# A graph layer over 1.65 million edges: every edge gathered in plain groups, no separate treatment of a node's edge to itself

## The chip, the cores and the metric

The kernel runs on one core of a Trainium2 chip. The metric is the device time of one execution in microseconds. The kernel before takes 18567.04 us, the median of 9 runs from 18510.53 to 18612.28 us. The engines are named as the profile names them: PE is the matrix engine (PEld its loading of weights), DVE the vector engine, ACT the scalar engine, POOL the engine that issues the indirect gathers, SP the one that issues most plain transfers.

## The reference, cut to what matters

There are 50,000 nodes of 160 numbers each (64 scalars and 32 three-vectors) and 1,650,000 edges sorted by their destination: 800,000 random pairs in both directions, and one edge from each node to itself. Because the sort is stable, a node's edge to itself is the last of its edges. Each edge has 4 attributes.

```python
ss, vv = (s[src], v[src])                  # the source's row of x
out0 = C0 * (ss * e0 @ W1 + dot * INV3 @ W2)
p3 = (ss @ W3)[:, :, None] * e1[:, None, :] * INV3
p4 = jnp.einsum('eui,uw->ewi', vv * e0[:, :, None], W4) * INV3
p5 = jnp.einsum('eui,uw->ewi', jnp.cross(vv, e1[:, None, :]), W5) * INV6
m = concat(out0, C1 * (p3 + p4 + p5))      # one message per edge
m_agg = segment_sum(m, dst, num_segments=n)
h = m_agg through Ws and Wv                # 160 x 160, block by block
x = layernorm(x + (x + relu(h)))
```

A message is linear in the source's row and linear in the four attributes. So the sum over a node's edges is the sum over k of (the sum of attribute k times the source's row) times a fixed 160 x 160 matrix, and the kernel gathers rows, forms these weighted sums by matrix products, and multiplies with the folded weights afterwards.

## The kernel before, in words

**Groups and pairs.** A group is `G` = 6 units of 128 edges, 768 edges, which touch at most `W` = 32 consecutive nodes. Two groups are a pair (`PG`), four a chunk (`QG`), twenty a super-group (`SG`). The main loop at the end of `tile_gnn_resnorm` runs over pairs, 1044 of them.

For each pair `gather` (line 319) issues 12 indirect transfers on POOL, one per unit, each of which brings 128 rows of x into the tile `xg`. The pool of `xg` has 4 buffers of one pair each: POOL can run 48 gathers ahead of the matrix products that read them, and then waits until PE has finished the oldest pair. `spread` (329) makes, on DVE, the weighted selection `ha` of 128 edges by 4 x 32 columns for each unit. `group_sums` (356) multiplies `ha` with the gathered rows into `ps` in PSUM, one matrix product per unit. A float32 product is two PE instructions and two weight loads in the records. `turn_sums` (370) transposes `ps` into `sums` on DVE.

**Behind a chunk.** `apply_weights` (598) multiplies a chunk's `sums` with the folded weights `BWk`, 5 products into `phc`, and ACT copies the result to `hp`. For each of 391 blocks of 128 nodes `block` (677) adds the chunks that touch it with 4 or 5 products by a 0/1 matrix into `phb`; then come the residual, the normalisation and the store. These products come from a task list, and `work` lets about one of them through after each gathered unit's product, so on PE they stand between the `ps` products in program order. Their PSUM tiles (`phc`, `phb`, `yx`, `ptx`) share one pool of two buffers.

**The edge of a node to itself.** Its row of x is the node's own, which is loaded in order anyway. From group 100 (`NH`) on the kernel therefore does not gather it. `pack` (431) reads rows of `L` = 790 edges, marks those whose source is their destination, and squeezes them out with predicated copies on DVE. The rest go to a DRAM array `edges` of 6 numbers an edge, and the attributes of the squeezed-out ones to an array `selves`, in 1994 stores of 18.5 KB and 1992 of 0.5 KB on SP. `load` (248) then reads super-groups from `edges` in one transfer of 360 KB. For every block, `ahead` (619) loads the rows of x and the stored attributes, `turned` (644) transposes the rows with two products into `ptx`, `own` (656) makes 8 products `yx` with the weights, and DVE adds them up into `t` with the attributes as factors; `block` adds `t` to `phb`. The first 100 groups are read from the inputs as they are (three transfers and a conversion on ACT), with the edges to itself among them.

**Order.** PE, DVE, ACT and SP keep the order in which the program writes their instructions. `after_pair` puts each step of later work at a pair: for a block whose last chunk ends at pair p, the load at p - 7 (`AHEAD`), `turned` at p - 4, `own` at p - 2, `block` at p + 4. At the end a few flags are read; if a group had spanned more than 32 nodes, a second, slower pass would follow.

```python
for j in range(n - len(others)):                     # gather, 319
    got.append(nc.gpsimd.indirect_dma_start(out=xg[:, j, :], ...).ins)
...
mm = nc.tensor.matmul(ps[:, j // G, :], ha[:, j].rearrange("p k w -> p (k w)"), xr, ...)   # group_sums, 356
```

Of the kernel before, what the change touches and what calls it, by code (L numbers as in the profile page):

```python
# [39 lines left out]
F32 = mybir.dt.float32  # L40
I32 = mybir.dt.int32
# [29 lines left out]
HELP = {}  # L71
HEAD = 100
BP = 2
RP = 128
RS = 16
KM = 31

ROWS = {ET.SP: 32, ET.Activation: 16}


def plan(n_nodes, n_edges):

    nblk = 125
    assert n_nodes % nblk == 0
    assert W == FB
    nb = n_nodes // nblk
    again = 9

    per_unit = P * n_nodes / n_edges
    group = max(g for g in range(1, 17)  # L90
                if g == 1 or (g + 0.2) * per_unit + 1 + 5 * math.sqrt(g * per_unit * per_unit / P) <= W)
    head = math.ceil(min(HEAD, n_edges / (group * P)) / SG) * SG
    eh = head * group * P
    row = group * P + math.floor(per_unit * group * (1 - n_nodes / n_edges))
    assert row * n_nodes / n_edges + 5 * math.sqrt(row * n_nodes / n_edges / 16) < KM

    far = math.ceil(6 * math.sqrt(n_edges) / 2 * n_nodes / n_edges) + 2
    rows = math.ceil((n_edges - eh) / row) + 2
    ngroups = math.ceil((n_edges - n_nodes + eh * n_nodes / n_edges + far) / (group * P))
    assert eh + (rows - 1) * row - n_nodes + eh * n_nodes / n_edges - far >= ngroups * group * P  # L100
    units = P * math.ceil(max(math.ceil(n_edges / P) + again - 1, math.ceil((eh + rows * row + 1) / P)) / P)
    return nblk, nb, again, group, units, ngroups, row, head, rows, far
# [3 lines left out]
def tile_gnn_resnorm(ctx: ExitStack, tc: tile.TileContext, x, src, dst, attr, W1, W2, W3, W4, W5, Ws, Wv, out, n_edges):  # L106
    nc = tc.nc
    N = x.shape[0]
    NBLK, NB, GA, G, NU, NG, L, NH, NR, FAR = plan(N, n_edges)
    NCH = math.ceil(NG / QG)  # L110
    EH = NH * G * P
# [94 lines left out]
    def near(c):  # L206
        p = c * QG * G * P
        return p / degree if p <= EH else EH / degree + (p - EH) / (degree - 1)

    step = QG * G * P / (degree - 1)  # L210
    cuts = sorted({0, NH // QG, NCH} | {round(i * NCH / 10) for i in range(10)})
    bounds = []
    for c0, c1 in zip(cuts, cuts[1:]):
        t = min((near(c) / N for c in range(c0, c1 + 1)), key=lambda t: abs(t - 0.5))
        off = 5 * math.sqrt(n_edges * max(0, t * (1 - t))) / (degree - 1) + 10
        bounds += [(-off, 0.75 * step + W + off)] * (c1 - c0)
# [9 lines left out]
    with tc.tile_pool(name="once", bufs=1) as once, tc.tile_pool(name="raw", bufs=2) as rawp, \  # L226
            tc.tile_pool(name="idx", bufs=2) as idxp, tc.tile_pool(name="rows", bufs=4) as rowp, \
            tc.tile_pool(name="far", bufs=3) as farp, \
            tc.tile_pool(name="ops", bufs=3) as op, tc.tile_pool(name="sums", bufs=4) as sump, \
            tc.tile_pool(name="hp", bufs=alive + 4) as hpp, tc.tile_pool(name="node", bufs=3) as np_, \  # L230
            tc.tile_pool(name="ahead", bufs=5) as aheadp, tc.tile_pool(name="outs", bufs=3) as outp, \
            tc.tile_pool(name="psC", bufs=1, space=PSUM) as psC, tc.tile_pool(name="psK", bufs=2, space=PSUM) as psK, \
            tc.tile_pool(name="psP", bufs=1, space=PSUM) as psP, tc.tile_pool(name="psA", bufs=2, space=PSUM) as psA, \
# [11 lines left out]
        offsets = {}  # L245
        evict = nc.vector.tensor_copy if ET.Activation in HELP else nc.scalar.copy

        def load(s):
# [3 lines left out]
            if g0 >= NH:  # L252
                p0 = g0 * G * P - EH
                r6 = rawp.tile([P, P, 2 + NK], F32, name="r6")
                dq.dma_start(r6[:n].rearrange("u p c -> u (p c)"),
                             edges[0, p0 * (2 + NK):(p0 + n * P) * (2 + NK)].rearrange("(u q) -> u q", u=n))
                return s, n, None, r6[:n, :, 0], r6[:n, :, 1], r6[:n, :, 2:]
# [6 lines left out]
            return s, n, ri, None, None, ra[:n]  # L264

        def cast(loaded):
            s, n, ri, sf, df, af = loaded
            if ri is not None:
                rf = rawp.tile([P, 2, P], F32, name="rf")
                begun.append(nc.scalar.copy(rf[:n], ri[:n]))  # L270
                sf, df = rf[:n, 0, :], rf[:n, 1, :]
            if HELP:

                ro = rawp.tile([P, P], I32, name="ro")
                nc.scalar.mul(ro[:n], sf, 4.0 * D)
                offsets[s] = ro
            return s, n, sf, df, af
# [41 lines left out]
        def gather(placed, u, n, others):  # L319

            xg = rowp.tile([P, PG * G, D], F32, name="xg")
            got = []
            for j in range(n - len(others)):
                got.append(nc.gpsimd.indirect_dma_start(  # L324
                    out=xg[:, j, :], out_offset=None, in_=x,
                    in_offset=bass.IndirectOffsetOnAxis(ap=placed[0][:, u + j:u + j + 1], axis=0)).ins)
            return [xg[:, j, :] for j in range(n - len(others))] + others, got
# [28 lines left out]
        def group_sums(p, rows, ha):  # L356
# [3 lines left out]
            rows, got = rows  # L360
# [13 lines left out]

        halves = ((0, L // 2), (L // 2, L))
        C = 2 + NK
        npacks = math.ceil(NR / RP)
        real = math.ceil((n_edges - EH) / L)
        LW = math.ceil(L / W) * W

        def row_start(r):

            lo, hi = (math.floor(r * L * (1 - 1 / degree)) - 2 * FAR - 2, math.ceil(r * L * (1 - 1 / degree)) + 2 * FAR + 2)
            return (max(lo, 0), hi if r else 0), (max(math.floor((EH + r * L) / degree) - FAR - 2, 0),
                                                  math.ceil((EH + r * L) / degree) + FAR + 2)

        edges = dram.tile([1, (row_start(NR - 1)[0][1] + L) * C], F32, name="edges")
        selves = dram.tile([1, (row_start(NR - 1)[1][1] + W) * NK], F32, name="selves")
        edge_bytes = edges.bitcast(U8).rearrange("o f -> (o f)")
        self_bytes = selves.bitcast(U8).rearrange("o f -> (o f)")  # L390
        rows_stored = [0]

        def row_table(tmp):

            NT = npacks * RP
            raw = tmp.tile([1, NT], I32, name="raw")
            at = tmp.tile([1, NT], F32, name="at")
            node = tmp.tile([1, NT], F32, name="node")
            nc.vector.memset(raw[:, NR:], 0)
            with nc.allow_non_contiguous_dma(reason="one number of each row"):  # L400
                dq.dma_start(raw[:, :NR], dst[EH:EH + NR * L].rearrange("(o r e) -> o r e", o=1, e=L)[:, :, 0])

            nz = math.ceil((row_start(0)[1][1] + W) / P)
            zeros = tmp.tile([P, nz * NK], F32, name="zeros")
            nc.vector.memset(zeros, 0.0)
            dq.dma_start(selves[0, 0:P * nz * NK].rearrange("(p f) -> p f", p=P), zeros)
            nc.gpsimd.iota(at, pattern=[[L, NT]], base=0, channel_multiplier=0, allow_small_or_imprecise_dtypes=True)
            most, least = math.ceil(EH / degree) + FAR, max(math.floor(EH / degree) - FAR, 0)
            nc.vector.tensor_scalar(node, raw, float(N), float(-most), op0=ALU.min, op1=ALU.add)
            nc.vector.scalar_tensor_tensor(node, at, 1 / degree, node, op0=ALU.mult, op1=ALU.min)  # L410
            nc.vector.tensor_scalar(node, node, float(most - least), None, op0=ALU.add)
            nc.vector.scalar_tensor_tensor(node, at, 1 / degree, node, op0=ALU.mult, op1=ALU.max)
            nc.vector.tensor_scalar(node, node, float(least), None, op0=ALU.add)

            nc.vector.tensor_copy(spots[:, :NT], node)
            nc.vector.tensor_copy(node, spots[:, :NT])

            nc.vector.scalar_tensor_tensor(at, at, node[:, 0:1], node, op0=ALU.add, op1=ALU.subtract)

            moved = raw.bitcast(F32)  # L420
            nc.vector.scalar_tensor_tensor(moved[:, :NR], raw[:, :NR], float(N), node[:, :NR],
                                           op0=ALU.min, op1=ALU.subtract)
            nc.vector.tensor_reduce(strayed[0:1, 0:1], moved[:, :NR], axis=AX.X, op=ALU.min)
            nc.vector.tensor_reduce(strayed[0:1, 1:2], moved[:, :NR], axis=AX.X, op=ALU.max)
            by_round = spots.rearrange("o (c j t i) -> o c j t i", c=npacks, j=RS, t=2)
            for t, (what, width) in enumerate(((at, C), (node, NK))):
                nc.vector.tensor_scalar(by_round[:, :, :, t, :],
                                        what.rearrange("o (c i j) -> o c j i", c=npacks, j=RS), float(4 * width), None,
                                        op0=ALU.mult)

        def pack(c):

            r0 = c * RP
            n = min(RP, NR - r0)
            e0 = EH + r0 * L
            e = slice(e0, e0 + n * L)
            steps, T = [], {}

            def read():
# [658 lines left out]
```

## Time and profile before

| What | Value |
|---|---|
| median of 9 runs | 18567.04 us |
| the profiled execution, its time | 18546.95 us |
| its span, first to last instruction | 18544.8 us |
| gathers on POOL | 12522, 946 ns busy each |
| first and last gather's start | 8.4 and 18502.2 us |
| PE matrix products, records | 41633, of them `ps` 25044, `yx` 6256, `phc` 5220, `phb` 3474, `ptx` 782 |
| DVE busy | 6445.8 us |
| ACT busy | 486.5 us |
| mean granted PE clock | 0.667 of full speed |

The profile is one execution taken by the hardware profiler. Its page gives busy times by engine, the chain of work that ended last, and groups of like instructions. Other views are drawn from the same trace: the waits (who sat idle, and what ended it), one tile's instructions, and the timeline. The span has no stages that differ: between 1000 and 18000 us every stretch of 2000 us holds between 1343 and 1374 POOL instructions. "Remote" in a wait means that the profile found no instruction whose end fits the semaphore that was waited for.

### The profile page before, as it was taken

The page shows a single profiled execution, that of the slowest core. Times are in us where ns is not written, and L with a number is a line of the kernel's source. Part 1 is how long each engine was busy: PE and PEld are TensorE (multiplying, and loading weights), DVE is VectorE, ACT ScalarE, POOL GpSimd, SP SyncE. Part 2 cuts the span into 40 slices and gives each one's busy share as a digit, 9 for nine tenths or more (in the row PEclk, how much of TensorE's full clock was granted, in tenths as well). Part 3 has the DMA queues.
Part 4 walks back from the last instruction along what each step waited for, and adds up shares of the span by engine and source line. Part 5 has one row for each costly group of instructions (what it writes and reads, how often), then busy time and mean ns, then how long its engine had stood idle before and what let it go on. Part 6 is the DMA issues. An engine that isn't in the chain of part 4 may idle for free.

```text
span 18544.8 us, 122717 instructions
## 1 busy us (share of the span) xinstructions
PE 8636.7 (47%) x41633; PEld 7739.0 (42%) x41634; DVE 6445.8 (35%) x11070; ACT 486.5 (3%) x1392; POOL 11853.4 (64%) x12536
## 2 busy tenths in 40 slices
PE   4444444444444454544445444454444445444444
PEld 3334444443444444444344444444444344444434
DVE  4332433423333242332333334233342423323322
ACT  0000000000000000000000000000000000000000
POOL 6666666666666666666666666666666666666665
PEclk6666666666666666666666666666666666666666
DMA  2222222222222222222222222222222222222222
GB/s 69 71 61 71 63 65 68 62 71 60 66 68 64 71 63 66 69 64 68 61 66 69 62 70 63 73 62 66 69 63 70 61 71 62 62 69 60 65 62 54
DMA packets 797538, 1215.93 MB, mean 66 GB/s; under 512 B 271491, under 2 KB 575800, under 8 KB 792918
## 3 DMA queue, kind: packets, MB, share of 16 engines
q0 software_dynamic: 601056, 1026.60, 22.5%
q1 hardware_dynamic: 194410, 180.15, 3.3%
q8 instruction: 330, 5.41, 0.1%
q14 instruction: 302, 2.47, 0.0%
q10 hardware_dynamic: 1440, 1.29, 0.0%
HBM read 1135.77 MB, written 71.40 MB: 65 GB/s over the span
## 4 chain that ended last, share of the span: by engine, by line
another core or an unknown queue 41%; issue 18%; PE 16%; DVE 10%; POOL 9%; DMA 1%; ACT 1%; DVEq 0%; SPq 0%; ACTq 0%; POOLq 0%
POOL xg L324 9%; PE ps L362 9%; DVE ha L336 2%; PE phb L684 2%; PE phc L603 2%; PE yx L665 2%; DVE hot L333 1%; DVE sums L372 1%; DMA xg<-in_x,si 1%; DVE prow L534 1%; DVE t L673 1%; DVE hot L638 0%; DVE pra L534 0%; DVE t L671 0%
## 5 line engine op out<-in xcount | busy, mean ns | idle before, releaser
L324 POOL DMA_INDIRECT xg<-in_x,si x12522 | 11849.2, 946 | 6649.1 <-issue 3633.5
L362 PE MATMUL ps<-xg,ha 128*128 128x160 f32 x25044 | 6542.7, 364 | 3452.6 <-issue 3115.2
L362 PEld LDWEIGHTS ps<-xg,ha 128*128 128x128 f32 x25044 | 5115.2, 241 | 3905.0 <-issue 3516.2
L372 DVE STREAM_TRANSPOSE sums<-ps 128x320 f32<-128x320 f32 x1044 | 533.7, 511 | 5392.0 <-remote 4064.8
L665 PE MATMUL yx<-BWh,xT 80*128 80x160 f32 x6256 | 1798.6, 365 | 881.7 <-issue 825.3
L684 PE MATMUL phb<-hp,hot 128*128 128x160 f32 x3474 | 1127.5, 415 | 2183.0 <-ACT xT L653 985.1
L603 PE MATMUL phc<-BWk,sums 128*128 128x160 f32 x5220 | 1354.2, 343 | 1203.5 <-DVE t L673 702.6
L336 DVE TENSOR_TENSOR ha<-hot,pk 128x1536 f32<-128x1536 f32 x1044 | 1829.9, 1753 | 35.7
L684 PEld LDWEIGHTS phb<-hp,hot 128*128 128x128 f32 x3474 | 836.3, 275 | 2297.3 <-ACT xT L653 1028.9
L665 PEld LDWEIGHTS yx<-BWh,xT 80*128 80x128 f32 x6256 | 1351.1, 242 | 1005.1 <-issue 942.9
L603 PEld LDWEIGHTS phc<-BWk,sums 128*128 128x128 f32 x5220 | 1018.4, 224 | 1264.1 <-DVE t L673 738.2
L673 DVE SCALAR_TENSOR_TENSOR t<-yx,sa,t 128x160 f32<-128x160 f32 x1173 | 449.4, 383 | 2150.3 <-remote 1657.8
L671 DVE TENSOR_SCALAR t<-yx,sa 128x160 f32<-128x160 f32 x391 | 148.6, 380 | 2056.8 <-remote 1831.2
L650 PE MATMUL ptx<-ident,xt 128*80 128x128 f32 (+1 forms) x782 | 202.6, 351 | 1230.0 <-DVE t L673 879.2
L686 DVE TENSOR_TENSOR phb<-phb,t 128x160 f32<-128x160 f32 x391 | 127.8, 327 | 1723.2 <-remote 954.3
L650 PEld LDWEIGHTS ptx<-ident,xt 128*80 128x80 f32 (+1 forms) x782 | 92.4, 142 | 1310.1 <-DVE t L673 936.3
L333 DVE TENSOR_TENSOR hot<-bank,rel 128x384 f32<-128x384 f32 x1044 | 551.0, 528 | 39.3 <-PE ps L362 28.8
L534 DVE COPY_PREDICATED prow<-marks,prow 128x2370 f32<-128x2370 int32 (+8 forms) x160 | 445.2, 2783 | 1.2
L607 ACT COPY hp<-phc 128x160 f32<-128x160 f32 x522 | 152.5, 292 | 9942.7 <-remote 5095.2
L653 ACT COPY xT<-ptx 80x256 f32<-80x256 f32 x391 | 143.6, 367 | 7944.4 <-remote 4721.4
L534 DVE COPY_PREDICATED pra<-marks,pra 128x1580 f32<-128x1580 int32 (+8 forms) x160 | 306.6, 1916 | 0.0
L638 DVE TENSOR_TENSOR hot<-bank,rr 128x512 f32<-128x512 f32 (+2 forms) x391 | 293.3, 750 | 13.5
(144 smaller groups left out, 2787.1 us busy)
## 6 DMA issues: line engine op xcount, KB each, us to landing
xg<-in_x,si POOLq DMA_INDIRECT x12522
edges<-prow SPq DMA_DIRECT2D x1994, 18.5 KB
r<-edges SPq DMA_DIRECT2D x99, 360.0 KB
selves<-mine SPq DMA_DIRECT2D x1992, 0.5 KB
xt<-in_x SPq DMA_DIRECT2D x195, 160.0 KB
out<-o SPq DMA_DIRECT2D x195, 160.0 KB
pra<-in_attr SPq DMA_DIRECT2D x15, 1580.0 KB
pri<-in_src SPq DMA_DIRECT2D x15, 395.0 KB
```

Source lines behind the costliest of these rows:

```text
L324: got.append(nc.gpsimd.indirect_dma_start(out=xg[:, j, :], out_offset=None, in_=x, in_offset=bass.IndirectOffsetOnAxis(ap=placed[0][:, u + ...
L333: nc.vector.tensor_tensor(hot[:, :n], slotsP[:, 0:W].unsqueeze(1).to_broadcast([P, n, W]), rel[:, u:u + n].unsqueeze(2).to_broadcast([P, n ...
L336: nc.vector.tensor_tensor(ha[:, :n], hot[:, :n].unsqueeze(2).to_broadcast([P, n, NK, W]), pk[:, :, u:u + n].rearrange("p k u -> p u k").un ...
L362: mm = nc.tensor.matmul(ps[:, j // G, :], ha[:, j].rearrange("p k w -> p (k w)"), xr, start=j % G == 0, stop=j % G == G - 1)
L372: nc.vector.transpose(at[:, :, i:i + ng, :].rearrange("p b g w -> p g b w"), ps[:, :ng].rearrange("p g (b f) -> p g b f", f=FB))
L534: nc.vector.copy_predicated(what[:n, a:e], mi[:, r].unsqueeze(2).to_broadcast([n, e - a, what.shape[2]]), what[:n, a + d:e + d])
L603: wrote("misc", nc.tensor.matmul(ph[:ng * W], at[:, b, :ng].rearrange("p g w -> p (g w)"), BWk[:, b, :], start=b == 0, stop=b == ND - 1))
L638: nc.vector.tensor_tensor(hot2[:, :len(cs)], slotsP.unsqueeze(1).to_broadcast([P, len(cs), P]), rr[:, :len(cs)].unsqueeze(2).to_broadcast( ...
L650: wrote("misc", nc.tensor.transpose(pt[:, i, :nb], xt[:nb, i * H:(i + 1) * H], ident[:nb, :nb]))
L665: wrote("misc", nc.tensor.matmul(y[:nb, k], xT[:, i, :nb], BWh[:, i, 2 * h + k, :], start=i == 0, stop=i == 1))
L673: nc.vector.scalar_tensor_tensor(t[:nb], y[:nb, i], sa[:nb, k:k + 1], t[:nb], op0=ALU.mult, op1=ALU.add)
L684: wrote("misc", nc.tensor.matmul(ph[:nb], hot2[:r, i, :nb], hp[:r], start=i == 0, stop=i == len(cs) - 1))
```

## The change

All 1,650,000 edges become plain groups in their order. There are 2149 groups instead of 2087, in 1075 pairs, 538 chunks and 108 super-groups, and 12,894 gathers instead of 12,522. Gone are `pack` and everything it uses (the row table, its marks in PSUM, the arrays `edges` and `selves` and the stores to them), `turned`, `own` and the addition of `t`. Every super-group is loaded as the first 100 groups were, with three transfers and one conversion on ACT. Rows of x are loaded 2 pairs before a block's last chunk ends instead of 7, as nothing but the residual needs them, in a pool of 4 buffers instead of 5. Unused code for gathers from other engines goes as well.

On the engines' programs, DVE goes from 11,244 instructions to 7,279 and SP from 4,000 small stores to none; PE loses 3128 `yx` and 782 `ptx` products, gains 372 `ps` and 80 `phc`, and has 1757 `phb` products, where it had 1737.

```diff
-    head = math.ceil(min(HEAD, n_edges / (group * P)) / SG) * SG
-    eh = head * group * P
-    row = group * P + math.floor(per_unit * group * (1 - n_nodes / n_edges))
...
-    ngroups = math.ceil((n_edges - n_nodes + eh * n_nodes / n_edges + far) / (group * P))
+    ngroups = math.ceil(n_edges / (group * P))
...
     def near(c):
         p = c * QG * G * P
-        return p / degree if p <= EH else EH / degree + (p - EH) / (degree - 1)
+        return p / degree
...
         def load(s):
-            if g0 >= NH:
-                p0 = g0 * G * P - EH
-                r6 = rawp.tile([P, P, 2 + NK], F32, name="r6")
-                dq.dma_start(r6[:n].rearrange("u p c -> u (p c)"),
-                             edges[0, p0 * (2 + NK):(p0 + n * P) * (2 + NK)].rearrange("(u q) -> u q", u=n))
-                return s, n, None, r6[:n, :, 0], r6[:n, :, 1], r6[:n, :, 2:]
             e = slice(g0 * G * P, (g0 * G + n) * P)
             ri = rawp.tile([P, 2, P], I32, name="ri")
             ra = rawp.tile([P, P, NK], F32, name="ra")
             dq.dma_start(ri[:n, 0, :], src1[e].rearrange("(u p) o -> u (p o)", p=P))
             dq.dma_start(ri[:n, 1, :], dst1[e].rearrange("(u p) o -> u (p o)", p=P))
             dq.dma_start(ra[:n].rearrange("u p k -> u (p k)"), attr[e].rearrange("(u p) k -> u (p k)", p=P))
...
-        def pack(c):
...
-        def turned(b, xt, sa):
-            for i in range(2):
-                wrote("misc", nc.tensor.transpose(pt[:, i, :nb], xt[:nb, i * H:(i + 1) * H], ident[:nb, :nb]))
-                yield 0.75
...
-        def own(b, xt, sa, xT):
-            for h in range(NK // 2):
-                y = psM.tile([P, 2, D], F32, name="yx", tag="misc")
-                for k in range(2):
-                    for i in range(2):
-                        wrote("misc", nc.tensor.matmul(y[:nb, k], xT[:, i, :nb], BWh[:, i, 2 * h + k, :], ...))
-                        yield 1
-                for i in range(2):
-                        nc.vector.scalar_tensor_tensor(t[:nb], y[:nb, i], sa[:nb, k:k + 1], t[:nb], ...)
...
-        def block(b, xt, t, hot2):
+        def block(b, xt, hot2):
...
-            nc.vector.tensor_tensor(ph[:nb], ph[:nb], t[:nb], op=ALU.add)
             return norm1(np_, ph[:nb], xt[:nb], nb)
...
-        AHEAD = 7
+        AHEAD = 2
...
-                after_pair(max(at - AHEAD + 3, START), do_turned, b)
-                after_pair(max(at - AHEAD + 5, START + 2), do_own, b)
```

## The prediction

> **What bounds the kernel now.** I read the page first, then POOL's waits, then the tile `xg`, then PE's timeline. The page:
>
> ```profile
> span 18544.8 us, 122717 instructions
> ...
> PE 8636.7 (47%) x41633; PEld 7739.0 (42%) x41634; DVE 6445.8 (35%) x11070; ACT 486.5 (3%) x1392; POOL 11853.4 (64%) x12536
> ...
> L324 POOL DMA_INDIRECT xg<-in_x,si x12522 | 11849.2, 946 | 6649.1 <-issue 3633.5
> L362 PE MATMUL ps<-xg,ha 128*128 128x160 f32 x25044 | 6542.7, 364 | 3452.6 <-issue 3115.2
> ...
> L665 PE MATMUL yx<-BWh,xT 80*128 80x160 f32 x6256 | 1798.6, 365 | 881.7 <-issue 825.3
> ```
>
> No engine is full by busy time. POOL comes nearest: a gather takes 946 ns and, in the undisturbed timeline, 0.30 us of issue follows, so one starts every 1.25 us. 12,522 x 1.25 = 15,653 us, with 8 us before the first and 43 us after the last start 15,704. The span is 2,841 us longer. POOL's own waits name the difference:
>
> ```profile
> POOL xg L324 <- PE ps L362: 1635.6, 257, 16.5
> POOL xg L324 <- remote: 1198.9, 302, 6.6
> ```
>
> Columns: us in total, times, longest. These 2,834 us fall, 600 times, on the first gather of a pair: POOL has filled its four `xg` buffers and waits for PE to give one back. Sorting the trace's starts by gather shows who is late: the rows have landed 2.2 to 2.3 us after their issue (middle half of the gathers), but PE's product with them starts 28 to 60 us after the issue, in 98% of cases. PE never stands at its data; it is always two to four pairs behind. So PE's in-order stream sets the rate, one pair per 17.75 us on average, against 15.0 us (12 x 1.25) on POOL. That PE is busy for only 47% is explained by its timeline:
>
> ```profile
> 2437.61 0.29 PEld L362 LDWEIGHTS ps<-xg,ha 128*128 128x128 f32 x1 [1.81 <-issue]
> 2439.00 0.43 PE L362 MATMUL ps<-xg,ha 128*128 128x160 f32 x1 [1.67 <-issue]
> 2439.70 0.29 PEld L665 LDWEIGHTS yx<-BWh,xT 80*128 80x128 f32 x1 [1.81 <-issue]
> 2440.40 0.43 PE L665 MATMUL yx<-BWh,xT 80*128 80x160 f32 x1 [0.97 <-issue]
> ...
> 2442.11 0.94 POOL L324 DMA_INDIRECT xg<-in_x,si  x1 [4.58 <-remote]
> ```
>
> ```profile
> 8037.01 3.04 PEld L362 LDWEIGHTS ps<-xg,ha 128*128 128x128 f32 x22
> 8037.14 3.15 PE L362 MATMUL ps<-xg,ha 128*128 128x160 f32 x22
> ```
>
> In the second stretch 22 products take 3.15 us, 0.14 us each. In the first, one product and its weight load need 1.4 to 2.1 us, with no wait on anything, and POOL sits 4.6 us for it. Such **slow stretches** (starts 0.7 or 1.4 us apart, five or more in a row) are found 367 times, 12.6 us in the median, 4,758 us together. Finished products can also show late:
>
> ```profile
> 14212.24 0.43 PE L362 MATMUL ps<-xg,ha 128*128 128x160 f32 x2
> ...
> 14217.38 0.74 PE L362 MATMUL ps<-xg,ha 128*128 128x160 f32 x2
> ...
> 14237.17 0.81 DVE L673 SCALAR_TENSOR_TENSOR t<-yx,sa,t 128x160 f32<-128x160 f32 x2 [20.29 <-remote]
> ```
>
> The `yx` products before 14212 reach DVE at 14237, and ACT and PE stand behind it. A "remote" wait in this one-core program is such a late report from PE, so the 41% "another core or an unknown queue" of the chain of waits is PE too. A slow stretch is likelier the more PE did before it: outside of them, one starts within 2 us in 1 to 2% of cases with under 30 product records in the 12 us before, in about 10% with over 50. I do not know the mechanism; load seems to bring it on.
>
> **The change part by part.**
>
> *More gathers.* 12,894 - 12,522 = 372 x 1.25 = **+465 us** on POOL, if POOL sets the rate. The floor is then 12,894 x 1.25 = 16,117, with the 51 us of start and tail **16,168 us**.
>
> *Own products gone.* PE loses 6,256 `yx` and 782 `ptx` records and gains 744 `ps`, 160 `phc`, 40 `phb` and some 24 for the added super-groups: 41,633 to about 35,560, -15%. By the price at full rate (0.14 us) the loss of 7,038 is only 1 ms. What they cost in PE's stream is in its pairs: 652 pairs in which no `yx` falls take 12.57 us on average, 389 with 16 of them 26.47 us. That is 0.87 us a record; fitted beside the other products it is 0.77 from single pairs and 0.52 to 0.62 over two or three neighbours, which share a slow stretch. There are 6.0 `yx` and 0.75 `ptx` a pair, so 6.75 x 0.52 to 0.87 = 3.5 to 5.9 us come off 17.75: 11.9 to 14.2 us. I take 0.62, the fit over three pairs, which leaves **13.5 us** a pair; the pairs with none, 12.57, say the same. Both are under 15.0.
>
> *What is late next.* POOL. At 13.5 against 15.0 us PE keeps up on average, but single pairs do not (12.57 has a spread of 8 us, 5% of them take over 29), and four buffers absorb 60 us. Laying the measured pair times, scaled to 13.5, in random order behind a supply of one pair per 15 us with four buffers leaves 150 to 450 us of waiting; at 12.6 it is 0 to 120, at 14.2 300 to 750, at 15.0 650 to 1,100. I take **280 us**.
>
> *`pack` gone.* Its copies on DVE and its stores on SP lie beside the work. In the 78 stretches of 100 us with none of its predicated copies POOL issued 67.0 gathers, in the 80 with seven or more 68.0. So its loss is put at 0; the ends are -100 us (PE's waits on DVE ahead of `phc` and `phb`, of which it is some part) and +100 (fewer pauses for PE). DVE keeps its per-pair work (0.5 + 0.5 + 1.75 us), well within 15 us.
>
> *Three loads and a conversion per super-group.* SP's three issues stand behind the store of `o`, which waits for DVE (8,640 us idle in total, harmless so far as nothing was due). The ACT conversion, queued one pair later, holds up `hp` and so `phb` until the data lands. Its price is the row of the first five super-groups: 407 ns, and what waited for it 3.1 us at most, except at the start. 103 more of them: 42 us on an engine 3% busy; ends 0 and 103 x 10 = 1,030 us if each held PE for 10 us. PE's slack of 60 us hides that; 0.
>
> *Rows loaded 2 pairs ahead, 4 buffers.* They are needed six pairs (90 us) after the load. 0.
>
> [...] The rows above have products at five to ten times 0.14 us, and PE 28 us behind its landed data. [...]
>
> **The sum.** 16,168 + 280 = 16,448 span; the time is 2 us over the span here: **16,450 us**, against the profiled 18,547 (the median shown is 20 us above that).
>
> **Rivals.**
>
> *A ceiling on PE's load (16,950).* In every 1000 us PE makes 2.15 to 2.32 product records per us. If something holds the mean there, after needs 35,560 / 2.245 = 15,840 us by count, hidden under POOL. But `yx` uses 80 of 128 rows and `ptx` moves half as much; counted so, before is some 38,900 records in 18,545 us, and 35,560 take 16,950. For it: uniform rate, slow stretches after load. Against: the pairs with `yx` cost far more than this weight.
>
> *The waits go with the gathers (19,100, slower).* If slow stretches belong to the full-height `ps` products and fill any room PE is given, each gather keeps its 2,843 / 12,522 = 0.227 us, and 12,894 x 1.477 + 51 = 19,095. It decides from where PE's pair stays above 17.2 us (1075 x 17.2 + 51 = 18,540), that is, if more than three quarters of the 5 us removed come back. For it: denser `ps` without the pauses at DVE means more load in short time, which brings slow stretches on. Against: the 652 pairs at 12.57.
>
> *PE follows its data at once (16,200).* Without backlog there are no bursts and hardly a slow stretch: the floor alone. Against: the start's folding of the weights puts PE 20 us behind at once, as now.
>
> *A second pass over the edges* if a plain group spans over 32 nodes: 768 edges at 33 a node are 23 nodes, and the first 100 groups are such already. Well over 20,000; hardly to be expected.
>
> **How the numbers follow.** POOL-bound with some waiting, 16,200 to 16,900: 0.55, likeliest 16,450. The ceiling, 16,800 to 17,500: 0.20. Follows at once: 0.05. The waits stay, 18,540 to 19,300: 0.18. Second pass or else: 0.02. The range 16,170 to 17,500 holds the first three, 0.8. What a measurement tells from no change is 0.2%, 37 us: faster 0.80, same 0.01, slower 0.19.
>
> **What would show it.** After, POOL's waits for `ps` and remote are below 600 us, PE's products start a few us after landing in many pairs, PE has some 35,560 records, and the gather's 946 ns stand. Wrong: PE still over 28 us behind everywhere and POOL waiting 2,800 us; a gather that is longer than 946 ns; PE waiting at L300 for late loads.

## The result, and the profile after

The changed kernel takes 18458.58 us (median of 10 runs, 18452.96 to 18464.26), the kernel before beside it 18560.46 us (31 runs, 18510.53 to 18612.28). The ratio is 0.9945, with a 95% interval of 0.9935 to 0.9954: faster by 0.55%. The forecast had the sign, and 11% where there is half a percent.

The page of the changed kernel, with its span, the busy times, and the rows of the gathers and of the group products:

```profile
span 18462.5 us, 97275 instructions
...
PE 7768.6 (42%) x35563; PEld 6672.4 (36%) x35564; DVE 3982.3 (22%) x7105; ACT 278.0 (2%) x1040; POOL 12192.9 (66%) x12906
...
L292 POOL DMA_INDIRECT xg<-in_x,si x12894 | 12191.2, 945 | 6237.8 <-issue 3770.3
L329 PE MATMUL ps<-xg,ha 128*128 128x160 f32 x25788 | 6468.9, 364 | 7234.5 <-issue 6407.4
```

The work is what the prediction counted: 35,563 records on PE, 12,894 gathers of 945 ns. What did not follow is the idle time of the products: the `ps` row stood idle for 3,453 us before and for 7,235 us now. POOL's waits for a free buffer, in us, times and the longest:

```profile
POOL xg L292 <- remote: 1273.0, 307, 6.8
POOL xg L292 <- PE ps L329: 1056.3, 189, 10.0
```

They were 2,834 us and are 2,329 us; I had put them at 280. Measured as what all gathers stand apart beyond 1.25 us, they went from 2,853 to 2,318 us. So the sum closes: 16,168 us of floor and 2,318 us of waiting are 18,486, against a span of 18,462. POOL lost 465 us to the 372 added gathers, as computed, and won back 535 us of waiting. PE still starts the products of a gather 19 to 54 us after its issue (1st to 99th percentile; before 28 to 61).

### The profile page after: what moved, and what is told of

Read it like the earlier page. It is cut to its first block, busy times and chain, and to the rows that moved or that the text cites. A ratio compares the mean times of both kernels' runs of the same rounds, so it can differ in the third digit from the quotient of the medians.

```text
span 18462.5 us, 97275 instructions
## 1 busy us (share of the span) xinstructions
PE 7768.6 (42%) x35563; PEld 6672.4 (36%) x35564; DVE 3982.3 (22%) x7105; ACT 278.0 (2%) x1040; POOL 12192.9 (66%) x12906
## 4 chain that ended last, share of the span: by engine, by line
issue 35%; POOL 32%; PE 18%; another core or an unknown queue 13%; DMA 2%; DVE 1%; SPq 0%; ACT 0%; POOLq 0%; DVEq 0%
POOL xg L292 32%; PE ps L329 13%; PE phc L347 2%; DMA xg<-in_x,si 2%; PE phb L389 2%; DVE ha L304 0%; PE pk L274 0%; DVE sums L339 0%; DVE hot L378 0%; PE bank L269 0%; DVE hot L301 0%; PE bank L270 0%; DVE st L172 0%; DVE y L170 0%
## 5 line engine op out<-in xcount | busy, mean ns | idle before, releaser
L292 POOL DMA_INDIRECT xg<-in_x,si x12894 | 12191.2, 945 | 6237.8 <-issue 3770.3
L347 PE MATMUL phc<-BWk,sums 128*128 128x160 f32 x5380 | 1528.4, 357 | 1047.8 <-issue 1044.2
L347 PEld LDWEIGHTS phc<-BWk,sums 128*128 128x128 f32 x5380 | 1128.0, 234 | 1158.7 <-issue 1157.4
L170 DVE SCALAR_TENSOR_TENSOR y<-phb,xt 128x160 f32<-128x160 f32 x391 | 126.0, 322 | 2577.2 <-PE ps L329 1618.1
L378 DVE TENSOR_TENSOR hot<-bank,rr 128x640 f32<-128x640 f32 (+2 forms) x391 | 296.0, 757 | 13.4
L184 DVE TENSOR_SCALAR o<-y,mv,rstd 128x160 f32<-128x160 f32 x391 | 147.4, 377 | 14.3
L274 PE MATMUL pk<-ident,ra 120*128 120x120 f32 x432 | 144.5, 385 | 4.9 <-DMA ra<-in_attr 4.9
L172 DVE BATCH_NORM_STATS2 st<-y 128x6 f32<-128x160 f32 x391 | 128.0, 327 | 13.4
L179 ACT ACTIVATE rstd<-mv,eps_t 128x1 f32<-128x1 f32 x391 | 115.9, 296 | 29.3 <-DVE mv L174 24.7
L264 DVE TENSOR_SCALAR rowid<-baseB,pidx 32x5 f32<-32x5 f32 (+1 forms) x436 | 108.8, 250 | 8.5
```

The lines of the kernel that those rows point to most:

```text
L172: nc.vector.bn_stats(st[:n], y[:n])
L184: nc.vector.tensor_scalar(o[:n], y[:n], mv[:n, 0:1], rstd[:n], op0=ALU.subtract, op1=ALU.mult)
L274: begun.append(nc.tensor.transpose(pk[:, k, :n], af[:, :, k], ident[:n, :n]))
L292: nc.gpsimd.indirect_dma_start(out=xg[:, j, :], out_offset=None, in_=x, in_offset=bass.IndirectOffsetOnAxis(ap=placed[0][:, u + j:u + j + ...
L347: wrote("misc", nc.tensor.matmul(ph[:ng * W], at[:, b, :ng].rearrange("p g w -> p (g w)"), BWk[:, b, :], start=b == 0, stop=b == ND - 1))
L378: nc.vector.tensor_tensor(hot2[:, :len(cs)], slotsP.unsqueeze(1).to_broadcast([P, len(cs), P]), rr[:, :len(cs)].unsqueeze(2).to_broadcast( ...
```

## The experiments

Each kernel ran with the kernel before beside it on the same chip; the chip's number is given. That turned out to matter more than anything else. "The record" is the measurement above, whose chip is not known.

### Four attempts to take the pauses from the changed kernel

`e1_zero_selection` compares against slots that never match, so every product has zeros as weights (all messages are left out). `e2_no_gathers` reads one fixed set of rows in place of the gathered ones. `e3_half_products` leaves out every second group product (half of the edges). `e4_no_first_backlog` is whole, but folds the weights ahead of the first gather.

```diff
 # e1: spread
-  slotsP[:, 0:W]
+  slotsP[:, 2 * W:3 * W]
 # e2: gather (fixed is loaded once, ahead of the loop)
-  for j in range(n):
-      nc.gpsimd.indirect_dma_start(out=xg[:, j, :], ...)
-  return [xg[:, j, :] for j in range(n)]
+  return [fixed[:, j, :] for j in range(n)]
 # e3: group_sums
+  if j % 2:
+      yield ps
+      continue
 # e4: ahead of the first place(cast(load(0)))
+  folded = weights(beginp, psM)
+  with tc.issue_after(folded):
+      ...
```

> The changed kernel with every selection tile ha all zero (it is compared with slots 64 to 95, which no edge has), so each group's sum is zero; every instruction, gather and shape stays, the products only multiply by zero. Theory 'load': PE is held back by what its products draw, so zeros take the slow stretches away and POOL sets the time, 16,170 to 16,300 us. Theory 'count': PE is held back by its number of products, whatever is in them: 18,460. Theory 'transfers': the slow stretches come from the gathered rows landing in SBUF: 18,460.

> The changed kernel without its gathers: the group products read one fixed tile of rows of x, loaded once; POOL has nothing to do, PE, DVE and ACT do all they did. It leaves the gathering out. Theories 'load' and 'count': PE goes on at its mean of 1.93 records a us, 35,563 / 1.93 = 18,400 us, slow stretches throughout. Theory 'transfers': without landing rows no slow stretches, PE at 0.14 to 0.27 us a record and waits of its own, 6,000 to 11,000 us.

> The changed kernel with the group products of every second unit left out; all gathers and all selections stay. 12,894 records fewer on PE, 22,670 left. Theories 'load' and 'count': at 1.93 a us 11,750 us, so POOL sets the time, 16,170 to 16,300. Theory 'transfers': the slow stretches stay as the landing rows do; PE's work in a pair falls by a third at most, 17,000 to 18,460.

> The changed kernel with the folding of the weights ahead of the first gather instead of behind the first pair, so that PE doesn't start 20 us behind. Theory 'bursts': slow stretches follow only when PE works off a backlog; without one it follows its data and POOL sets the time, 16,200 to 16,400. Theories 'load', 'count' (of the mean) and 'transfers': 18,460 to 18,500.

Measured on chip 1: 16162.19, 4899.65, 16155.92 and 16170.48 us. Three of the four sit on POOL's floor, 16,168 us, whatever was taken away. The kernel before beside them took **15736.96 us**, not 18,560. That is its own floor, 15,704 us. On this chip there was nothing to take away, so none of the four tells the theories apart. What `e2` does tell is what PE's whole work costs with no gathers beside it:

```profile
span 4897.9 us, 82867 instructions
...
PE 4868.1 (99%) x35563; PEld 4818.4 (98%) x35564; DVE 3943.9 (81%) x7105; ACT 269.6 (6%) x1040; POOL 1.7 (0%) x12
```

That is 4897.9 / 35,563 = 0.138 us a record, as in the undisturbed stretches of the kernel before (0.14).

### The changed kernel itself, on that chip

> The changed kernel itself, beside the kernel before, to see whether the difference of the last four runs, where the kernel before took 15,737 us, lies in the chip. 'The chip differs': if the kernel before takes some 15,740 us here, the changed one takes POOL's floor, 16,170 (+2.7%), with PE a few us behind its data; if it takes 18,560, the changed one takes 18,460. 'Something in the four kernels': the changed one takes 18,460 whatever the kernel before takes.

It takes 16191.74 us against 15736.96: 455 us **more** than the kernel before (one run of each; the kernel before is the run that stood beside the four). Its page, and POOL's wait for the products:

```profile
span 16190.0 us, 97275 instructions
...
L329 PE MATMUL ps<-xg,ha 128*128 128x160 f32 x25788 | 10112.7, 493 | 4531.8 <-DMA xg<-in_x,si 4485.7
```

```profile
POOL xg L292 <- PE ps L329: 196.0, 643, 0.3
```

Here PE's idle time is ended by the landing of `xg`, where it was "issue" in the record's profile. No wait of POOL for a product is longer than 0.3 us. PE starts the products 2.6 us after a gather's issue in the median, 4.0 us at the 99th percentile. The same instructions are bound by PE's lateness in one place and by POOL in the other. The granted clock does not tell the two places apart: it is 0.633 in the record's profile and 0.631 here (the kernel before has 0.667 and 0.664).

### Are the own products worth anything there?

`b1_without_own` is the kernel before without `turned`, `own` and the addition of `t` (the messages of squeezed-out edges are left out).

```diff
-  nc.vector.tensor_tensor(ph[:nb], ph[:nb], t[:nb], op=ALU.add)
...
-  after_pair(max(at - AHEAD + 3, START), do_turned, b)
-  after_pair(max(at - AHEAD + 5, START + 2), do_own, b)
```

> The kernel before without the own products: no turned, no own, t isn't added; packing, stores and loads stay. It leaves out the messages of the edges that are not gathered. On a chip where PE pauses (the kernel before at 18,560): the theory of the prediction, own products cost PE 3.5 to 5.9 us a pair, gives POOL's floor, 15,750 to 16,200; the rival, the pauses stretch until the same number of group products passes, gives 18,400 to 18,560. On a chip where it doesn't pause (15,737) both give 15,700 to 15,740.

15703.09 us (8 runs) against 15706.78 (9 runs) on chip 4, ratio 0.9998 (0.9987 to 1.0009). Where PE keeps in step, 7,038 records of own products cost nothing. `e4` ran once more, on chip 13, and gave the price of the change again:

> The kernel of e4_no_first_backlog again, in case it meets a chip on which PE pauses (the kernel before at 18,560 us). There 'bursts' gives 16,170 to 16,400 us, 'load' and 'count' 18,400 to 18,500. On a chip without pauses (15,710 to 15,740) it gives 16,170 again.

16210.58 us against 15706.54, 504 us or 3.2% more (one run of each).

### PE made dense on purpose

`x1_before_dense` and `x2_after_dense` put 25 further products ahead of each group's, 100 records a pair. `h1_act_helps` is the kernel before with one unit in 72 fetched by ACT, row by row, in place of POOL.

```diff
 # x1, x2: group_sums
+  for _ in range(25 if j % G == 0 else 0):
+      nc.tensor.matmul(ps[:, j // G, :], ha[:, j]..., xr, start=True, stop=True)
 # h1
-  HELP = {}
+  HELP = {ET.Activation: 72}
```

> The kernel before, with 25 further products with the same operands ahead of each group's (50 a pair, 100 records; each is overwritten, the sums stay). This makes PE the bound by plain work. Theory A (PE's work costs what it costs undisturbed, 0.136 us a record, and pauses belong to the chip or to the measurement, not to PE's load): 139.9 records a pair x 0.136 = 19.0 us, about 19,900 us in all, PE busy near 99%, POOL waiting for ps about 4,000 us in waits of a few us. Theory B (load on PE together with gathers brings the pauses on, as my prediction said): 100 records more at the rate of the recorded profile, 2.245 a us, add 44 us a pair; over 30,000 us, with stretches of starts 0.7 us apart. If this chip shows pauses in the kernel before itself (18,500 instead of 15,700), the same two numbers tell whether they grow with load.

> The changed kernel with the same 50 further products a pair. It shows what the own products are worth where PE is the bound. Theory A (a record costs its issue, 0.136 us): 133.1 records a pair x 0.136 = 18.1 us, 1075 pairs, about 19,460 us, ratio to the same kernel with own products about 0.98. My prediction's price (0.62 us a record, 6.75 records a pair): 4.2 us a pair less, ratio about 0.80.

> The kernel before with one unit in 72 gathered by 128 row transfers from ACT in place of POOL's indirect one (a path that the kernel before has, switched off). If POOL's 1.25 us a gather is the whole bound, 12,522 x 71/72 = 12,348 gathers x 1.25 + 51 = about 15,490 us, 1.4% under the kernel before on a chip without pauses (15,710). If ACT's row transfers hold back ACT's copies or the gathers' own transfers, no gain or slower. On a chip with pauses the difference drowns: PE's rate decides there.

They ran on chip 11, where the kernel before takes 18646.83 us (3 runs), so the pauses are there. Measured: 28174.35, 27473.09 and 20744.72 us (2 runs each). Neither theory of the pair had the number: A said 19,900 us, B over 30,000. PE makes 5.2 product records a us here, twice the rate that I had thought might be a ceiling. The 104,350 added records cost 9,528 us, 0.091 us each. Between the two dense kernels the ratio is 27473 / 28174 = 0.975, near A's 0.98 and far from my 0.80. In time it is 27.0 less 25.6 = 1.4 us a pair for 6.8 records, 0.21 us each: more than A's 0.136, a third of my 0.62. Where PE is slow shows in the timeline of `x1`:

```profile
12018.99 0.43 PE L687 MATMUL phb<-hp,hot 128*128 128x160 f32 x2
12019.26 1.93 PE L363 MATMUL ps<-xg,ha 128*128 128x160 f32 x13
...
12022.59 0.57 PE L363 MATMUL ps<-xg,ha 128*128 128x160 f32 x3 [1.40 <-issue]
12023.47 0.95 POOL L324 DMA_INDIRECT xg<-in_x,si  x1 [0.31 <-issue]
12024.71 0.30 PE L363 MATMUL ps<-xg,ha 128*128 128x160 f32 x1 [1.55 <-issue]
12025.42 0.54 PE L363 MATMUL ps<-xg,ha 128*128 128x160 f32 x2 [0.41 <-issue]
12026.84 5.87 PE L363 MATMUL ps<-xg,ha 128*128 128x160 f32 x31 [0.89 <-issue]
...
12035.97 0.95 POOL L324 DMA_INDIRECT xg<-in_x,si  x1 [11.55 <-PE ps L365]
```

The gather at 12023.47 is the last of twelve, which began at 12009.69. PE runs at full rate into them, becomes slow near their end, and is at full rate again 3.4 us after the last one was issued. This repeats through the execution. Sorted by the time since a burst of gathers began, gaps of 0.6 to 3 us between products make 2 of 6,252 us in its first 6 us, 80% of the time from 12 to 16 us, and some 20 us of over 9,000 from 18 us on. **PE's slow stretches are tied to the gathers, and end when the gathers stop.**

`h1` is 11% slower (ratio 1.1128, 1.1076 to 1.1179). 8,308 us of ACT's idle time ahead of `rstd` end with its row transfers (`xr`), and PE waits 2,393 us for late rows of `xt`. It does not help on such a chip; what it does on one bound by POOL was not seen.

### No backlog, on a chip with pauses

The dense kernels left two readings. Either a backlog makes the products dense, and dense products beside gathers bring the pauses (then a start without backlog would stay in step), or the two share something that fills up in any order. `f1_before_no_backlog` is the kernel before with the edit of `e4`.

> The kernel before, with its own messages, but with the weights folded ahead of the first gather (some 40 us later start of the gathers), so that PE begins without a backlog. Theory D (PE's pauses come when dense products meet running gathers, and a backlog makes the products dense, so that it feeds itself): on a chip where the kernel before takes 18,500 us, PE stays a few us behind the gathers and this takes about 15,750 us, 15% less. Theory S (gathers and products share something that is full on such a chip in any order): as before, 18,400 to 18,700. On a chip where the kernel before takes 15,710 it only adds its later start: 15,710 to 15,760.

> The changed kernel without the first backlog, once more. On a chip with pauses: theory D about 16,200 us, theory S about 18,450. On a chip without pauses 16,170 to 16,220 as in the two looks before, 2.9 to 3.2% over the kernel before.

Chip 0: 18576.69 and 18375.93 us, beside 18528.23 for the kernel before (one run each). Theory D falls: `e4` starts in step and pauses all the same. S stands so far. The start of `e4` on this chip:

```profile
56.24 0.95 POOL L293 DMA_INDIRECT xg<-in_x,si  x1 [0.30 <-issue]
56.32 0.90 PE L330 MATMUL ps<-xg,ha 128*128 128x160 f32 x2 [0.33 <-DMA xg<-in_x,si]
...
75.48 0.43 PE L330 MATMUL ps<-xg,ha 128*128 128x160 f32 x1 [2.37 <-issue]
76.24 0.95 POOL L293 DMA_INDIRECT xg<-in_x,si  x1 [0.30 <-issue]
77.49 0.95 POOL L293 DMA_INDIRECT xg<-in_x,si  x1 [0.30 <-issue]
78.28 0.43 PE L330 MATMUL ps<-xg,ha 128*128 128x160 f32 x1 [2.37 <-issue]
...
109.08 0.43 PE L330 MATMUL ps<-xg,ha 128*128 128x160 f32 x1 [2.37 <-issue]
115.44 0.52 DVE L340 STREAM_TRANSPOSE sums<-ps 128x320 f32<-128x320 f32 x1 [49.79 <-remote]
115.67 0.94 POOL L293 DMA_INDIRECT xg<-in_x,si  x1 [10.98 <-remote]
...
123.75 2.67 PE L330 MATMUL ps<-xg,ha 128*128 128x160 f32 x18
```

The first gather is at 14.84 us. Until 62 us PE follows the gathers, with two records in 1.25 us and no backlog (a short lag at 58 us is there on chip 13 too). It is late at 65.75, and from 68 us on it falls, to one record in 2.8 us from 72.68 on, while POOL goes on. POOL runs out of buffers after its gather of 103.75, stands for 11 us, and then PE does 18 records in 2.67 us. The same instructions on chip 13 (`e4_second_look`) go on undisturbed:

```profile
75.72 0.95 POOL L293 DMA_INDIRECT xg<-in_x,si  x1 [0.31 <-PE ps L330]
75.86 0.90 PE L330 MATMUL ps<-xg,ha 128*128 128x160 f32 x2 [0.32 <-DMA xg<-in_x,si]
```

Sorting each trace by how long the gathers have run without a break of over 3 us gives product records a us on PE:

| Gathers unbroken for | before | after | `e4`, chip 0 | `x1`, chip 11 |
|---|---|---|---|---|
| 4 to 8 us | 5.10 | 5.74 | 6.28 | 7.33 |
| 8 to 12 us | 3.99 | 5.12 | 5.43 | 4.62 |
| 12 to 16 us | 1.48 | 1.21 | 1.39 | 1.19 |
| 16 to 20 us | 0.74 | 0.65 | 0.71 | no such run |
| 20 to 30 us | 0.61 | 0.41 | 0.50 | no such run |

From 12 us on the columns agree although the kernels ask for very different amounts of PE's work: PE gets about 1.2 to 1.5 records a us, from 16 us on under 0.8. It gets its rate back only with a break: in the first three columns it is fast again (six records within 2 us) 5 to 6 us after the last gather in the median (the 14.5 us at the start of `e4` above are an exception). On chips 1 and 13 the changed kernel's gathers run for the whole execution without a break of 3 us, and PE makes 2.2 records a us beside them.

Time alone is not the condition, though. In the first stretch of `e4` PE stayed fast for 53 us. Its slow part has begun where four starts in a row are 0.6 to 4 us apart; up to there and for 20 us behind it the windows of the first stretch are, in `x1` (chip 11) and in the kernel before (the record):

```profile
7.70:26.70 19.00, 12.80 (x75) 0.96 0.23 61
26.70:46.70 20.00, 5.05 (x12) 0.50 0.25 67
```

```profile
8.40:55.30 46.90, 21.58 (x71) 0.98 0.31 76
55.30:75.30 20.00, 3.79 (x10) 0.50 0.52 97
```

The number behind the x is PE's product records. With dense work PE is slow after 19 us, with light work after 47, and both times some 70 records have been made since the gathers began: 74 and 70, by starts. `x2` has 69 after 18.7 us, the changed kernel on the record 70 after 47.3, `e4` on chip 0 80 after 53.2, and `h1`, on the chip of `x1`, 70 after 48.4. (`f1`'s first stretch ended after 47 records, before PE was slow.) In the later stretches the median is 66 records (before and after), 71 (`f1`), 74 (`e4`), 78 and 80 (`x1`, `x2`) and 50 (`h1`, with ACT's transfers beside the gathers), at median times of 10 to 18 us. **So PE's own records take part: beside running gathers it makes some 70, soon or late, before it becomes slow.** The times in the table agree, it seems, because PE comes out of every break with a backlog and works it off at a similar pace.

With this the waiting can be counted as breaks (POOL standing for over 0.75 us beyond its pace):

| | records on PE | breaks | mean break | records from break to break |
|---|---|---|---|---|
| before | 41,633 | 602 | 4.7 us | 69 |
| after | 35,563 | 496 | 4.6 us | 72 |
| `f1`, chip 0 | 41,633 | 576 | 4.9 us | 72 |
| `e4`, chip 0 | 35,563 | 432 | 5.1 us | 82 |

A stretch of gathers with its break lets PE do some 70 to 80 records, and POOL pays about 5 us for it. From the kernel before alone, 35,563 / 69 = 515 breaks of 4.7 us make 2,420 us of waiting after the change, against 2,318 measured; this was worked out after the result. It does not carry over to the dense kernels, where PE also works at full rate in the breaks: `x1` has 140 records and 11.8 us to a break, `x2` 134 and 10.5.

### Rows or gathers?

What the gathers take from PE may go by rows and bytes, or by gather. `k4_half_rows` gathers 64 rows in place of 128 and multiplies 64 (half of the edges is left out); `e3` ran with it, to show whether PE's own count takes part.

```diff
-  out=xg[:, j, :], ... ap=placed[0][:, u + j:u + j + 1]
+  out=xg[:P // 2, j, :], ... ap=placed[0][:P // 2, u + j:u + j + 1]
```

> The changed kernel with gathers of 64 rows in place of 128, and products over 64 rows; the other half of the edges is left out. As many gathers and product records, half the bytes and rows. On a chip with pauses (kernel before near 18,500): if what PE and the gathers share is used by rows or bytes, PE keeps in step and the time is POOL's floor, 16,170 us or less if a shorter gather is issued sooner; if it is used by the gather as such (its issue, its semaphores), the pauses stay and the time is near 18,400. On a chip without pauses: POOL's floor, which tells whether 1.25 us a gather depends on its rows.

> The changed kernel with every second group product left out (12,894 product records of 25,788; the rest of PE's work stays, some 22,700 records, 21 a pair). On a chip with pauses: if gathers alone set how long PE is slow, 18,300 to 18,460 as with all products; if PE's load takes part, its 36% fewer records let it stay in step, 16,200 us. In between, the share: by the phase table of x1 PE makes about 1.3 records a us while gathers have run for over 12 us, and 21 records in 15 us are 1.4, so I expect 16,200 to 17,000. On a chip without pauses 16,160 as in the first look.

They ran on chip 12, without pauses (before 15707.58 us): 15606.84 and 16154.29 us (one run each). Neither question is answered by them; that PE's count takes part is what the first stretches above show. One thing is answered: the row of the gathers in `k4`,

```profile
L292 POOL DMA_INDIRECT xg<-in_x,si x12894 | 11635.8, 902 | 3937.4 <-issue 3650.1
```

is 902 ns where 128 rows took 945. POOL's pace is 1.21 us with half the rows, 1.25 with all, so its floor is one of gathers, hardly of rows.

## Why the prediction was right and wrong

**More gathers: right.** +465 us was predicted. On the chips without pauses, where nothing covers it, the changed kernel is 455 us (chip 1) and, with the weights folded first, 434 us (chip 1) and 504 us (chip 13) above the kernel before; on the record it is inside the sum that closes.

**"This leaves 13.5 us a pair": the step that failed.** The pair takes 17.17 us (18462.5 / 1075) after 17.76. I priced a record of own products at 0.62 us, from a fit of pair times and from the 652 pairs that had none and took 12.57 us. In the changed kernel no pair has any. On chips with pauses a record is worth about 0.1 us, at most 0.2: 535 us of waiting less for 6,070 records less (0.088), 0.091 in `x1` against the kernel before, 0.107 between `f1` and `e4` on chip 0 (2,871 and 2,219 us of waiting), and 0.21 between `x1` and `x2`. On chips without pauses it is worth nothing (`b1`, 15703.09 against 15706.78 us). The fit compared pairs inside one regime and took a difference between pairs for the saving of removing what they held. PE's pace over time was set by a cycle of some 70 records and a break of the gathers; within that cycle some pairs fall into the fast part and some into the slow one. The changed kernel's pairs, all without own products, fit this: 12.9 us in the median, as short as the 12.57 us pairs before, but 17.2 in the mean, as 5% take over 42 us. That this is why the pairs without own products were short is my reading; that their price is not 0.62 us is measured. A record's share of a break, 4.7 us / 69 = 0.07 us, would have been near.

**"Load seems to bring it on": right, but it did not enter the sum.** Slow stretches begin after some 70 of PE's records beside running gathers, and end with a break of the gathers; in `e4` on chip 0 this holds for a kernel in step too. The sum took the pairs' times instead. The 367 slow stretches of 4,758 us are described too narrowly: with starts of 0.7 and 1.4 us alone there are about 100 of 520 us; with all gaps of 0.6 to 3 us, 2.1 and 2.8 us among them, 360 of 4,484 us.

**"POOL is late next, 280 us": wrong with it.** I laid pair times of 13.5 us in random order behind POOL's supply. They are neither 13.5 us nor random. With fewer records to a gather POOL runs longer before it stops (median unbroken stretch 24 gathers in both, the 90th percentile 36 in place of 24), and PE's slow part is longer by that, which refills the room: PE's gaps of over 0.6 us within a stretch without a break of 3 us are 23.6 us in the mean, 17.2 before.

**`pack`, loads, later rows at 0: no sign against it.** The floors, computed without a term for them, hold within 45 us on the chips without pauses.

**The rivals.** "The waits go with the gathers" (19,100) had the mechanism most nearly: the slow stretches fill the room that PE is given. It put the break-even at 17.2 us a pair, and the pair came to lie at 17.17, just under it. That the forecast has the sign of the record is luck. Its size was too high: a gather keeps 2,318 / 12,894 = 0.18 us of waiting, not 0.227, because the breaks fall with PE's records. The ceiling on PE's rate (16,950), as a mean that PE can't pass, is refuted by 5.2 records a us in `x1`. "Follows at once" (16,200) is what happens on chips 1 and 13.

**"PE 28 us behind its landed data": right where PE pauses.** On the record's measurement and on chips 0 and 11 PE was late; the changed kernel on the record still has it start the products 19 to 54 us after a gather's issue. On chips 1 and 13, where the change ran without pauses (2.6 us after the issue in the median of `c1`), the 465 us of the added gathers are about the whole difference (+455 and +504 us), with PE busy for 72% of the span in `c1` and POOL the bound. My error was not to take PE for late but to price its lateness by what stood in a pair, when it went by PE's records and the gathers together.

## What stays open

What it is that gathers and PE share, and why some chips have it and others not. No chip was met in both conditions, and only chip 1 on more than one occasion, so whether it belongs to the chip or to the occasion is not shown either. The kernel without gathers (`e2`) never ran where PE pauses. One more observation stands beside it. Each gather signals 16 times (206,323 in `c1`, for 12,894 gathers). Of these some 200,000 signals the traces hold 35,767 (before) and 35,474 (after) on the record and 28,618 to 51,750 in the runs on chips 0 and 11, but 200,330 to 206,328 in every run with gathers on chips 1, 4, 12 and 13. So wherever PE pauses, records of signals go missing, and the loss comes first: in `e4` on chip 0, the trace holds 41 of these signals in the 5 us from 20 us on, 12 in those from 30 us on and 7 in those from 45 us on, before PE falls behind at 62 us; chip 13's has 64 or more in each. Records are lost without pauses too: in `e2`, where PE is 99% busy, 2,837 of about 10,000 signals of PE are recorded (10,085 instructions of the changed kernel on PE signal). Of PE's own signals the trace of before holds 6,582 of 7,470. Where a record is missing, "remote" can also stand for a releaser that was not recorded, so that each such wait is a late report of PE, as the prediction has it, is not shown. What the lost records and the pauses have to do with each other no run here shows. `k4` and `e3` on a chip with pauses would have told whether rows or gathers count, and how far the pauses go when PE's records are cut; this wasn't seen.

Neither kernel is ahead on every chip. With pauses the changed kernel is 0.55% ahead (with the weights folded first 0.8%, one run), without them it is 3% behind.

## What to carry to other kernels

A price fitted between parts of one trace holds only while what sets the pace stays the same; before using it to predict a removal, ask what makes the slow parts begin and end, and sort the trace by that, not only by what was in them. Try more than one measure and a start with light work: by time the slow part seemed to come after 12 us of gathers, and only the first stretches, 19 against 47 us at the same 70 records, told time from count. When an engine is late with "issue" as the only cause and its busy rows can't explain it, look for what it goes with on the other engines, here POOL's gathers, and ask how much of the room that you make it fills: here 2,318 of 2,853 us of waiting stayed. And measure on more than one chip before calling a kernel bound by something: here the sign of the change depends on it.

## What was not expected of the hardware

- The kernel before takes 15,707 to 15,737 us on four chips (1, 4, 12, 13) and 18,528 to 18,647 us on two (0, 11), 18% more, with the same gather of 946 to 949 ns.
- On the second kind, PE becomes slow once it has made some 70 product records beside unbroken gathers, whether that takes 19 us (`x1`) or 53 (`e4` on chip 0), down to one record in 2.8 us (`e4`), and is at full rate again some 5 us after the last gather.
- An indirect gather of 64 rows takes POOL 902 ns, one of 128 rows 945 ns.
